# Two graph-attention and expert layers on one core: filled regions without pads, weight packing from the first block, early slots at 14 tiles, VectorE work of layer 1's routing moved, and the first norms in order

## The chip, the cores and the metric

The kernel runs on one core of one Trainium2 chip. The metric is the device time of one execution, in microseconds (us). Engines are named as the profile names them: PE (TensorE, the matmuls; PEld its weight loads), DVE (VectorE), ACT (ScalarE), POOL (GpSimd) and SP (SyncE, which here only issues DMAs). [...]

## The reference

x has N = 2708 rows (nodes) of D = 256 floats, adj is 2708 x 2708 (int32, about 1.2% ones). With E = 8 experts of hidden width 1024 in layer 0 and 512 in layer 1:

```python
# layer 0
h = layernorm(x)
q, k, v = h @ Wq.T + bq, h @ Wk.T + bk, h @ Wv.T + bv
x = x + elu(softmax(where(adj > 0, q @ k.T / 16, -9e15)) @ v)
h = layernorm(x); probs = softmax(h @ Wr + br)
# the two best experts of each row, weighted by their share of the two;
# each expert norms h once more: layernorm(h) * ln_g[e] + ln_b[e], then gelu MLP
x = x + sum_of_two(weight * expert(h))
# layer 1
H = layernorm(x) @ W_fc + b_fc
x = x + softmax(where(adj > 0, (H @ w_src)[:, None] + (H @ w_dst)[None] + b_att, -1e9)) @ H
h = layernorm(x); probs = softmax(h @ gate_w + gate_b)
x = x + sum_of_two(probability * expert(h))        # gelu MLP, no norm of its own
```

## The kernel before

The rows are cut into NT = 22 tiles of 128 (the last has 20 rows). Layer 0's attention takes queries in six blocks of four tiles (`BLOCKS`; the last is 148 rows) and walks the 22 key tiles k in each.

**Layer 0's attention** (`layer0_attention`). At the start the first four tiles are normed (`norm`: statistics on DVE L150 and L151, a scaling L152, a power on POOL L156, and the normed tile L160), transposed and multiplied with Wv (`prepare`), and the queries of block 0 are made (L331). Then for each block and k: `scores` (PE L345, plus the mask, already converted to `apart`, as an additive matmul L351), the exponential on ACT (L356), and the neighbour mask mT on DVE (L357, from the same scores, kept for layer 1); two steps later `attend` (L367). While block b runs, `load_mask` brings the int32 adjacency rows of block b+1 (SP, L254, four buffers, 0.35 MB each) and DVE turns each into `apart` (L257). In block 0 tiles 4 to 21 are normed and prepared on the way.

**Routing** (`Experts.route`, a generator that `Line.step` moves on by one stage at a time, so that a tile's routing runs in small pieces beside the attention of the next block). For each tile: statistics, the norm, a second copy of the row (L694), transposes, gate logits (L701), the two best (L709 to L726), a matmul that counts the rows already given to each expert (L730, L731), and two scatters on POOL that write the 128 rows into the experts' regions of `disp` in DRAM (L748; each row with its token number and weight). In layer 1 `finish` adds the bias to the residual on DVE (L526), and `evict` copies the accumulators alternately on DVE and ACT (L536).

**Experts.** A region's rows are cut into chunks of 128; a chunk is a slot. After `early` = 16 tiles are routed, `begin` places the first 24 slots (`FULL_AFTER`) among chunks that are surely full, and fetches the rows (SP, L889) and the weights (an indirect gather on POOL, L874, ring of four) of three slots ahead. Once all tiles are routed, `place(n, SLOTS)` numbers the rest. A chunk that isn't full must not pick up stale rows: before, each layer had a `disp` of its own, and `place` wrote 128 rows of `nobody` (token N, weight 0) behind the end of each of the eight regions, with register loads on SP:

```python
for e in range(E):
    at = nc.values_load(end[0:1, e : e + 1], ..., engines=(SP,))
    self.other_rows(nc.sync.dma_start(disp[bass.ds(at, P), :], nobody))
```

A slot (`slots`): transpose the rows (L913), first matmul (L933), gelu on ACT (L941), second matmul (L949), bias and weight on DVE (L955, L956), and a scatter with addition into the rows of the result on POOL (L957). The scatter of a slot waits until the one before has landed. 46 slots always run, two and then the rest only if the numbers need them.

**Packing** (`pack_weights`). Per expert the weights are copied DRAM to DRAM into one row per partition (2.2 MB in layer 0, 1.1 MB in layer 1). These copies, the idle rows of `disp` and later the reloading of mT are a list `background`, popped at fixed steps:

```python
if b > 0:
    if k % 5 == 1 and background:
        background.pop(0)()
    line.step()
```

**Order.** SP's instructions stand in the order of the program (`tc.manual_schedule(engines={SP})`); those of the other engines are ordered by a scheduler when the kernel is built. `prepare`, masks and constants compete there.

Of the kernel before, what the change touches and what calls it, by code (L numbers as in the profile page):

```python
# [41 lines left out]
FULL_AFTER = {16: 24}  # L42
# [13 lines left out]
def adj_ffn_kernel(ctx: ExitStack, tc: tile.TileContext, a: dict, out: bass.AP):  # L56
# [32 lines left out]
    part = const.tile([P, 1], F32, name="part")  # L89
    nc.gpsimd.iota(ints[:, :1], pattern=[[0, 1]], base=0, channel_multiplier=1)  # L90
    nc.vector.tensor_copy(part, ints[:, :1])
# [20 lines left out]

    def load_bcast(name, n, c0=0):
        t = const.tile([P, n], F32, name=f"{name}_b")
        nc.gpsimd.dma_start(t, a[name][c0 : c0 + n].partition_broadcast(P))
        return t
# [10 lines left out]
    def load_dmajor(pool, name, n, eng=None):  # L127
        t = pool.tile([P, DC, n], F32, name=f"{name}_w")
        (eng or nc.sync).dma_start(t, a[name].rearrange("(c p) n -> p c n", p=P))
        return t  # L130

    wr = load_dmajor(const, "L0_ffn_Wr", E, nc.gpsimd)
    wg = load_dmajor(const, "L1_ffn_gate_w", E, nc.gpsimd)

    wfc = const.tile([P, DC, D + 1], F32, name="wfc")
    nc.gpsimd.dma_start(wfc[:, :, :D], a["L1_gnn_W_fc"].rearrange("(c p) n -> p c n", p=P))
    for c in range(DC):
        junk = small.tile([P, D], F32, name="junk", bufs=1)
        nc.vector.scalar_tensor_tensor(
            junk, wfc[:, c, :D], 1.0, wdst_b,  # L140
            op0=ALU.mult, op1=ALU.mult, accum_out=wfc[:, c, D : D + 1],
        )

# [80 lines left out]
    def layer0_attention(line):  # L224
        with ExitStack() as scope, ExitStack() as until_last:
# [63 lines left out]
            with tc.tile_pool(name="fold", bufs=1, side="right") as fold:  # L289
# [7 lines left out]
                first = [norm(t) for t in range(4)]  # L297
# [99 lines left out]
            apart = mask_of(0)  # L397
            for t in range(4):
                prepare(t, first[t])
            for _ in load_mask(0, 0, apart):  # L400
                pass
            g = queries(0)
            late, total, accs = [], None, None
            for b, (b0, nb, ts_) in enumerate(BLOCKS):
# [6 lines left out]
                for k in range(NT):  # L411
                    if b == 0:
# [5 lines left out]
                        if k + 4 < NT:  # L418
                            prepare(k + 4, norm(k + 4))

# [19 lines left out]
                    if k >= 2:  # L440
                        next(later_mask, None)
                    if b > 0:
                        if k % 5 == 1 and background:
                            background.pop(0)()
                        line.step()
# [18 lines left out]
    def layer1_attention(mTs, line):  # L464
        with ExitStack() as scope:
# [7 lines left out]
            def load_x2(t):  # L473
                x2s[t] = rows.tile([P, D], F32, name="xin", bufs=9)
                nc.sync.dma_start(x2s[t][: ROWS[t]], xd0[t * P : t * P + ROWS[t], :])

# [45 lines left out]
            def finish(t, raw, total):  # L522
# [3 lines left out]
                nc.vector.tensor_add(x2[:r], x2[:r], bfc_b[:r])  # L526
# [6 lines left out]
            def evict(ts_, accs, total):  # L533
                for j, (t, acc) in enumerate(zip(ts_, accs)):
                    raw = rows.tile([P, D + 1], F32, name="raw", bufs=6)
                    (nc.scalar.copy if j % 2 else nc.vector.tensor_copy)(  # L536
                        raw[: ROWS[t]], acc[: ROWS[t]]
                    )
# [5 lines left out]
            for g, wide in enumerate(GROUPS):  # L544
# [4 lines left out]
                for k in range(NT + (LAG1 if g == 0 else 0)):  # L549
# [14 lines left out]
                    if 0 <= j < wide:  # L564
                        load_x2(ts_[j])
# [47 lines left out]
    class Experts:  # L613
        def __init__(self, layer, hidden, packed_weights, w_gate, gate_bias, own_norm, xd, disp, early):
# [12 lines left out]
            runs = [(0, 0, n // RING), (n, 0, -(-(SURE - n) // RING))]  # L627
            self.number = const.tile([P, SLOTS, 2], F32, name=f"number{layer}")
            number_i = const.tile([P, SLOTS], I32, name=f"number_i{layer}")
            for s0, c0, size in runs:  # L630
                nc.gpsimd.iota(
                    number_i[:, s0 : s0 + size * RING], pattern=[[1, size], [size, RING]], base=c0,
                    channel_multiplier=0,
                )
            s0 = n + runs[1][2] * RING
# [6 lines left out]
            )  # L642

# [30 lines left out]
        def route(self, t, x):  # L674
# [3 lines left out]
            r = ROWS[t]  # L678
            rows2 = [routing.tile([P, DROW], F32, name=f"row{j}") for j in range(2)]
# [14 lines left out]
            nc.vector.tensor_copy(rows2[1][:r, : D + 1], rows2[0][:r, : D + 1])  # L694
# [60 lines left out]
        def place(self, s0, s1):  # L755
# [8 lines left out]
            if all_chunks:  # L764

                end = one.tile([P, E], I32, name="end")
                nc.vector.tensor_add(end, n_e, regions)
                for e in range(E):
                    at = nc.values_load(
                        end[0:1, e : e + 1], min_val=e * CAP, max_val=e * CAP + N,  # L770
                        engines=(mybir.EngineType.SP,),
# [308 lines left out]
```

The softmax here doesn't subtract the row's maximum and nothing guards it: scores larger than these inputs give would overflow.

## Time and profile before

| what | value |
|---|---|
| median of three runs | 1418.88 us (1417.09 to 1419.42) |
| profiled execution | 1421.76 us, its span 1420.0 us |
| PE busy | 1292.1 us (91%), granted clock 0.964 on the mean |
| DVE, ACT, POOL busy | 569.7, 348.9, 435.3 us |
| DMA | 203.01 MB, mean 143 GB/s; SP's queue 107.86 MB, POOL's 93.73 MB |

The span runs from the first to the last instruction. The stages, by the starts and ends of their instructions: until 35 us the first norms, values and queries; until 548 layer 0's attention (blocks end near 137, 228, 322, 419, 505 and 548); until 890 layer 0's slots; from 905 to 1130 layer 1's attention with the routing of its first tiles; then layer 1's slots, in the first of which the last tiles are routed; the last scatter starts at 1404 and the output is copied behind it. PE is busy through most of this, so for a part of the change what matters is whether PE waits at that place, and for what.

### The profile page before, as it was taken

The numbers are of one execution on the slowest core, as the hardware profiler recorded it, in microseconds if no ns is written. First come the engines' busy times: TensorE is split into PE (matmuls) and PEld (weight loads), VectorE is DVE, ScalarE is ACT, GpSimd is POOL, SyncE is SP. The second block draws the span as 40 slices with busy tenths as digits, with TensorE's granted clock in tenths as the row PEclk, the third lists the DMA queues.
The fourth block names the chain that finished last, engine by engine and source line by source line (L and its number), as shares of the span: only waits on it lengthen the run. The fifth ranks groups of instructions, "written<-read, shape, count | busy, mean of one in ns | idle before, by whom it ended". The sixth has DMA issues, their size and how long they took to land. (4 is left out here: it accounts for less than half of the span.)

```text
span 1420.0 us, 21606 instructions
## 1 busy us (share of the span) xinstructions
PE 1292.1 (91%) x7680; PEld 1009.8 (71%) x7680; DVE 569.7 (40%) x2182; ACT 348.9 (25%) x1035; POOL 435.3 (31%) x478
## 2 busy tenths in 40 slices
PE   5999999999999999999999999599989876989872
PEld 3676666666566666999999999478878565878662
DVE  5623744536417264422221222565465543323220
ACT  2322222122112224433333332232001142222120
POOL 5100110110101122543333333431333346555552
PEclk8999999999999999999999999899999978999996
DMA  7601785978727036556686543310221256564664
GB/s 238 207 4 42 205 203 148 248 181 226 190 71 169 23 132 241 156 169 201 203 297 198 155 123 100 81 32 12 65 79 54 73 177 154 114 170 106 183 185 105
DMA packets 108620, 203.01 MB, mean 143 GB/s; under 512 B 25197, under 2 KB 83861, under 8 KB 101933
## 3 DMA queue, kind: packets, MB, share of 16 engines
q1 hardware_dynamic: 76172, 107.86, 27.0%
q0 software_dynamic: 32336, 93.73, 23.0%
q8 instruction: 63, 1.03, 0.3%
q14 instruction: 49, 0.39, 0.1%
HBM read 261.27 MB, written 69.41 MB: 233 GB/s over the span
## 5 line engine op out<-in xcount | busy, mean ns | idle before, releaser
L949 PE MATMUL acc<-ring,hT 128*128 128x256 f32 x1120 | 279.4, 386 | 24.8 <-ACT hT L941 24.8
L933 PE MATMUL mm<-xe,ring 128*128 128x128 f32 x2240 | 286.0, 283 | 9.7 <-DVE xe L923 4.7
L933 PEld LDWEIGHTS mm<-xe,ring 128*128 128x128 f32 x2240 | 275.9, 198 | 23.9 <-issue 14.0
L941 ACT ACTIVATE hT<-mm,ring 128x128 f32<-128x128 f32 x560 | 159.6, 368 | 376.8 <-issue 292.7
L949 PEld LDWEIGHTS acc<-ring,hT 128*128 128x128 f32 x1120 | 200.0, 192 | 55.9 <-ACT hT L941 34.6
L345 PE MATMUL s<-g,xnT 128*128 128x512 f32 (+1 forms) x440 | 215.2, 605 | 4.9 <-DVE mT L357 4.9
L367 PE MATMUL acc<-v,p 128*128 128x257 f32 (+1 forms) x880 | 216.9, 390 | 0.0
L957 POOL DMA_INDIRECT xd<-y,xg x94 | 149.1, 1586 | 173.5 <-DVE y L955 61.1
L517 PE MATMUL acc<-parts,mT 128*128 128x257 bf16 (+1 forms) x1452 | 175.7, 274 | 1.5 <-POOL parts L504 1.0
L955 DVE TENSOR_TENSOR y<-acc,bias 128x256 f32<-128x256 f32 x94 | 39.8, 424 | 339.1 <-PE acc L949 286.6
L367 PEld LDWEIGHTS acc<-v,p 128*128 128x128 f32 (+1 forms) x880 | 159.7, 192 | 19.2
L517 PEld LDWEIGHTS <-mT 128*128 128x128 fp8e4 (+1 forms) x1452 | 137.4, 98 | 30.6 <-issue 9.7
L748 POOL DMA_INDIRECT disp<-row,to x88 | 86.4, 982 | 235.7 <-DVE to L745 139.2
L874 POOL DMA_INDIRECT ring<-L_ffn_packed,weight_row x99 | 104.4, 1055 | 157.9 <-issue 102.9
L156 POOL TENSOR_TENSOR ln_rs<-ln_rs,minus_half 128x2 f32<-128x2 f32 x88 | 66.8, 779 | 245.9 <-DVE ln_rs L152 198.6
L357 DVE TENSOR_SCALAR mT<-s 128x512 fp8e4<-128x512 f32 x110 | 75.4, 687 | 150.4 <-ACT p L356 149.2
L345 PEld LDWEIGHTS s<-g,xnT 128*128 128x128 f32 (+1 forms) x440 | 77.1, 187 | 58.4 <-issue 45.9
L356 ACT ACTIVATE p<-s 128x512 f32<-128x512 f32 x110 | 65.0, 594 | 192.3 <-PE s L351 192.3
L351 PEld LDWEIGHTS <-apart 128*128 128x128 fp8e4 (+1 forms) x440 | 34.2, 99 | 64.5 <-issue 64.5
L257 DVE TENSOR_SCALAR apart<-adj 128x677 fp8e4<-128x677 int32 x80 | 40.9, 515 | 54.2 <-DMA adj<-in_adj_dram 53.7
L913 PE MATMUL tp<-ident,xg 128*128 128x128 f32 x188 | 39.3, 279 | 20.3 <-DMA xg<-disp 17.2
L166 PE MATMUL misc<-ident,xn 128*128 128x128 f32 (+1 forms) x132 | 27.5, 290 | 23.4 <-DVE ln_rs L152 11.6
(183 smaller groups left out, 1067.7 us busy)
## 6 DMA issues: line engine op xcount, KB each, us to landing
adj<-in_adj_dram SPq DMA_DIRECT2D x84, 338.5 KB
L_ffn_packed<-in_L_ffn_W_dram SPq DMA_DIRECT2D x16, 1024.0 KB
xg<-disp SPq DMA_DIRECT2D x99, 129.0 KB
L_ffn_packed<-in_L_ffn_W_dram SPq DMA_DIRECT2D x16, 512.0 KB
neighbours<-mT SPq DMA_DIRECT2D x5, 1408.0 KB
mT<-neighbours SPq DMA_DIRECT2D x5, 1408.0 KB
xin<-in_x_dram SPq DMA_DIRECT2D x42, 128.0 KB
xd<-x SPq DMA_DIRECT2D x42, 128.0 KB
```

Source lines behind the costliest of these rows:

```text
L156: nc.gpsimd.tensor_tensor(rs[:r, 1], rs[:r, 0], minus_half[:r], ALU.pow)
L345: nc.tensor.matmul(ps[:kr, :nb], xnT[:, c, k0 : k0 + kr], g[:, c, :nb], start=(c == 0), stop=False,)
L356: nc.scalar.activation(p[:kr, :nb], ps[:kr, :nb], AF.Exp, scale=1.0 / 16.0)
L357: nc.vector.tensor_scalar(mT[:kr, k, :], ps[:kr, :nb], -BIG / 2, None, ALU.is_gt, saturate=False,)
L367: nc.tensor.matmul(accs[j][:r], p[:kr, j * P : j * P + r], v[:kr, k, :], start=(k == 0), stop=(k == NT - 1),)
L517: nc.tensor.matmul(acc[:r], mT[:, k, q0 : q0 + r], parts[:, k, i], start=(k == 0 and i == 0), stop=(k == NT - 1 and i == 2),)
L748: nc.gpsimd.indirect_dma_start(disp[:], bass.IndirectOffsetOnAxis(ap=to[:r, j : j + 1], axis=0), rows2[j][:r], None,)
L874: nc.gpsimd.indirect_dma_start(w, None, packed[:], bass.IndirectOffsetOnAxis(ap=self.weight_row[:, s : s + 1], axis=0), bounds_check=E * P ...
L933: nc.tensor.matmul(ps[:, i, :], w[:, c * hidden + f * P : c * hidden + (f + 1) * P], xe[:, c, :], start=(c == 0), stop=(c == DC - 1),)
L941: nc.scalar.activation(hT[:, f, :], ps[:, i, :], AF.Gelu, bias=w[:, b1 + f : b1 + f + 1])
L949: nc.tensor.matmul(ps, hT[:, f, :], w[:, w2 + f * D : w2 + (f + 1) * D], start=(f == 0), stop=(f == hc - 1),)
L957: start = nc.gpsimd.indirect_dma_start(xd[:], bass.IndirectOffsetOnAxis(ap=xg.bitcast(I32)[:, D : D + 1], axis=0), y, None, compute_op=ALU ...
```

## The change

Five things, in one version.

1. **Filled regions without pads.** One `disp` serves both layers. In layer 0, `fill(i)` writes `nobody` into tile row i of all eight regions (1.06 MB) on SP: tiles 0 to 3 in block 0 (k from 18), the others one by one when tiles are routed (tile t fills t + 4). The pads are gone. In layer 1 the regions still hold layer 0's rows; `mark_rows` works out which rows of a late slot lie behind the end, and the slot's scatter then takes token and weight from a small tile `to` (slots from 20 on).
2. **Weight packing from the first block.** `background` is popped in block 0 at k = 8, 10, ... 20, and afterwards at k % 5 == 1 as before.
3. **Layer 1's early slots at 14 tiles** instead of 16, 20 slots instead of 24. The second run of slots in both layers is numbered downwards.
4. **VectorE work of layer 1's routing moved.** The residual's bias is added on POOL when the residual is loaded, the row copy goes to ACT, and all evictions go to ACT.
5. **First norms in order.** The first four norms, the loads of the constants and the first mask are put in the order of the program on DVE and POOL too; the loads of the constants are collected in a list and come behind the norms.

```diff
@@ -39,7 +39,7 @@
-FULL_AFTER = {16: 24}
+FULL_AFTER = {16: 24, 14: 20}
@@ -86,9 +86,12 @@
     ints = const.tile([P, 1 + E], I32, name="ints")
-    part = const.tile([P, 1], F32, name="part")
+    part = const.tile([P, 3], F32, name="part")
     nc.gpsimd.iota(ints[:, :1], pattern=[[0, 1]], base=0, channel_multiplier=1)
-    nc.vector.tensor_copy(part, ints[:, :1])
+    nc.vector.tensor_copy(part[:, 0:1], ints[:, :1])
+    nc.vector.tensor_scalar(part[:, 1:2], part[:, 0:1], -1.0, -float(N), op0=ALU.mult, op1=ALU.add)
+    nc.vector.tensor_scalar(part[:, 2:3], part[:, 0:1], float(N), None, ALU.add)
@@ -110,9 +113,14 @@
+    constants = []
...
         t = const.tile([P, n], F32, name=f"{name}_b")
-        nc.gpsimd.dma_start(t, a[name][c0 : c0 + n].partition_broadcast(P))
+        constants.append(
+            partial(nc.gpsimd.dma_start, t, a[name][c0 : c0 + n].partition_broadcast(P))
+        )
@@ -124,22 +132,27 @@
-    def load_dmajor(pool, name, n, eng=None):
+    def load_dmajor(pool, name, n):
         t = pool.tile([P, DC, n], F32, name=f"{name}_w")
-        (eng or nc.sync).dma_start(t, a[name].rearrange("(c p) n -> p c n", p=P))
+        nc.sync.dma_start(t, a[name].rearrange("(c p) n -> p c n", p=P))
...
-    wr = load_dmajor(const, "L0_ffn_Wr", E, nc.gpsimd)
-    wg = load_dmajor(const, "L1_ffn_gate_w", E, nc.gpsimd)
+    wr = const.tile([P, DC, E], F32, name="wr")
+    wg = const.tile([P, DC, E], F32, name="wg")
     wfc = const.tile([P, DC, D + 1], F32, name="wfc")
-    nc.gpsimd.dma_start(wfc[:, :, :D], a["L1_gnn_W_fc"].rearrange("(c p) n -> p c n", p=P))
-    for c in range(DC):
-        junk = small.tile([P, D], F32, name="junk", bufs=1)
-        nc.vector.scalar_tensor_tensor(
-            junk, wfc[:, c, :D], 1.0, wdst_b,
-            op0=ALU.mult, op1=ALU.mult, accum_out=wfc[:, c, D : D + 1],
+    for to, name in ((wr, "L0_ffn_Wr"), (wg, "L1_ffn_gate_w"), (wfc[:, :, :D], "L1_gnn_W_fc")):
+        constants.append(
+            partial(nc.gpsimd.dma_start, to, a[name].rearrange("(c p) n -> p c n", p=P))
...
+    def dst_column():
+        for c in range(DC):
+            junk = small.tile([P, D], F32, name="junk", bufs=1)
+            nc.vector.scalar_tensor_tensor(
+                junk, wfc[:, c, :D], 1.0, wdst_b,
+                op0=ALU.mult, op1=ALU.mult, accum_out=wfc[:, c, D : D + 1],
+            )
@@ -294,7 +307,17 @@
                     load_x(t)
-                first = [norm(t) for t in range(4)]
+                with tc.manual_schedule(
+                    engines={mybir.EngineType.DVE, mybir.EngineType.Pool}
+                ):
+                    first = [norm(t) for t in range(4)]
+                    for start in constants:
+                        start()
+                    apart = mask_of(0)
+                    for _ in load_mask(0, 0, apart):
+                        pass
+                dst_column()
@@ -394,11 +417,8 @@
-            apart = mask_of(0)
...
                 prepare(t, first[t])
-            for _ in load_mask(0, 0, apart):
-                pass
@@ -417,6 +437,8 @@
                             prepare(k + 4, norm(k + 4))
+                    if b == 0 and k >= NT - GROUP:
+                        experts0.fill(k - (NT - GROUP))
@@ -439,9 +461,9 @@
                         next(later_mask, None)
+                    if background and (k >= 8 and k % 2 == 0 if b == 0 else k % 5 == 1):
+                        background.pop(0)()
                     if b > 0:
-                        if k % 5 == 1 and background:
-                            background.pop(0)()
@@ -473,6 +495,11 @@
                 nc.sync.dma_start(x2s[t][: ROWS[t]], xd0[t * P : t * P + ROWS[t], :])
+                return x2s[t]
+            def load_residual(t):
+                x2 = load_x2(t)[: ROWS[t]]
+                nc.gpsimd.tensor_add(x2, x2, bfc_b[: ROWS[t]])
@@ -523,7 +550,6 @@
                 yield
-                nc.vector.tensor_add(x2[:r], x2[:r], bfc_b[:r])
@@ -531,11 +557,9 @@
             def evict(ts_, accs, total):
-                for j, (t, acc) in enumerate(zip(ts_, accs)):
+                for t, acc in zip(ts_, accs):
                     raw = rows.tile([P, D + 1], F32, name="raw", bufs=6)
-                    (nc.scalar.copy if j % 2 else nc.vector.tensor_copy)(
-                        raw[: ROWS[t]], acc[: ROWS[t]]
-                    )
+                    nc.scalar.copy(raw[: ROWS[t]], acc[: ROWS[t]])
@@ -562,7 +586,7 @@
                     if 0 <= j < wide:
-                        load_x2(ts_[j])
+                        load_residual(ts_[j])
@@ -624,15 +648,17 @@
             n = FULL_AFTER[early]
-            runs = [(0, 0, n // RING), (n, 0, -(-(SURE - n) // RING))]
+            size = -(-(SURE - n) // RING)
+            runs = [(0, 0, n // RING, 1), (n, size - 1, size, -1)]
...
             number_i = const.tile([P, SLOTS], I32, name=f"number_i{layer}")
-            for s0, c0, size in runs:
+            for s0, c0, size, step in runs:
                 nc.gpsimd.iota(
-                    number_i[:, s0 : s0 + size * RING], pattern=[[1, size], [size, RING]], base=c0,
-                    channel_multiplier=0,
-                )
-            s0 = n + runs[1][2] * RING
+                    number_i[:, s0 : s0 + size * RING], pattern=[[step, size], [size, RING]],
+                    base=c0, channel_multiplier=0,
+                )
+            s0 = n + size * RING
@@ -640,6 +666,15 @@
+        def fill(self, i):
+            regions_ = self.disp[:IDLE, :].rearrange("(e t p) d -> p e t d", e=E, p=P)
+            start = nc.sync.dma_start(
+                regions_[:, :, i], nobody.unsqueeze(1).to_broadcast([P, E, DROW])
+            )
+            tc.declare_no_dep(start.ins, group=self.groups[0], reason="other rows of disp")
@@ -676,6 +711,8 @@
             r = ROWS[t]
+            if own_norm and t + GROUP <= NT:
+                self.fill(t + GROUP)
@@ -691,7 +728,9 @@
             )
-            nc.vector.tensor_copy(rows2[1][:r, : D + 1], rows2[0][:r, : D + 1])
+            (nc.vector.tensor_copy if own_norm else nc.scalar.copy)(
+                rows2[1][:r, : D + 1], rows2[0][:r, : D + 1]
+            )
@@ -761,17 +800,6 @@
             nc.vector.tensor_copy(n_e, ps[:, :E])
-            if all_chunks:
-                end = one.tile([P, E], I32, name="end")
-                nc.vector.tensor_add(end, n_e, regions)
-                for e in range(E):
-                    at = nc.values_load(
-                        end[0:1, e : e + 1], min_val=e * CAP, max_val=e * CAP + N,
-                        engines=(mybir.EngineType.SP,),
-                        skip_runtime_bounds_check_because="an expert has at most N tokens",
-                    )
-                    self.other_rows(nc.sync.dma_start(disp[bass.ds(at, P), :], nobody))
@@ -809,6 +837,21 @@
                 )
+            marked = all_chunks and not self.own_norm
+            if marked:
+                end = one.tile([P, E], F32, name="end")
+                change_end = one.tile([P, E - 1], F32, name="change_end")
+                passed_end = one.tile([P, n, E], F32, name="passed_end")
+                nc.vector.tensor_add(end, n_e, regions)
+                nc.vector.tensor_sub(change_end, end[:, 1:], end[:, : E - 1])
+                nc.vector.tensor_mul(
+                    passed_end[:, :, : E - 1], passed[:, :, : E - 1],
+                    change_end.unsqueeze(1).to_broadcast([P, n, E - 1]),
+                )
+                nc.vector.tensor_copy(
+                    passed_end[:, :, E - 1 :], end[:, 0:1].unsqueeze(1).to_broadcast([P, n, 1])
+                )
@@ -820,6 +863,8 @@
                 nc.vector.tensor_scalar(self.used, last[:, E - 1 : E], float(s0), None, ALU.add)
+                if marked:
+                    self.mark_rows(s0, passed_end, row)
@@ -850,6 +895,22 @@
                 op0=ALU.mult, op1=ALU.add,
+            )
+        def mark_rows(self, s0, ends, row):
+            n = SLOTS - s0
+            left = self.one.tile([P, n], F32, name="left")
+            self.has = self.one.tile([P, n], I32, name="has")
+            self.instead = self.one.tile([P, n, 2], I32, name="instead")
+            nc.vector.tensor_reduce(left, ends, AX.X, ALU.add)
+            nc.vector.tensor_sub(left, left, row)
+            nc.vector.tensor_scalar(left, left, part[:, 0:1], None, ALU.is_gt)
+            nc.vector.tensor_scalar(self.has, left, -1.0, None, ALU.mult)
+            nc.vector.memset(self.instead, 0)
+            nc.vector.tensor_scalar(
+                self.instead[:, :, 0], left, part[:, 1:2], part[:, 2:3], op0=ALU.mult, op1=ALU.add
@@ -953,10 +1014,20 @@
                 nc.vector.tensor_add(y, ps, bias2)
-                nc.vector.tensor_scalar(y, y, xg[:, D + 1 : D + 2], None, ALU.mult)
+                to = xg.bitcast(I32)[:, D : D + 2]
+                if not own_norm and s >= FULL_AFTER[self.early]:
+                    i = s - FULL_AFTER[self.early]
+                    to = two.tile([P, 2], I32, name="to", bufs=3)
+                    nc.vector.tensor_tensor(
+                        to, xg.bitcast(I32)[:, D : D + 2],
+                        self.has[:, i : i + 1].to_broadcast([P, 2]), ALU.bitwise_and,
+                    )
+                    nc.vector.tensor_tensor(to, to, self.instead[:, i], ALU.bitwise_or)
+                nc.vector.tensor_scalar(y, y, to.bitcast(F32)[:, 1:2], None, ALU.mult)
...
                     xd[:],
-                    bass.IndirectOffsetOnAxis(ap=xg.bitcast(I32)[:, D : D + 1], axis=0),
+                    bass.IndirectOffsetOnAxis(ap=to[:, 0:1], axis=0),
@@ -1013,13 +1084,12 @@
-    disps = [dram.tile([E * CAP + P, DROW], F32, name=f"disp{i}") for i in range(2)]
-    for disp in disps:
-        background.append(partial(nc.sync.dma_start, disp[IDLE:, :], nobody))
+    disp = dram.tile([E * CAP + P, DROW], F32, name="disp")
+    background.append(partial(nc.sync.dma_start, disp[IDLE:, :], nobody))
...
     packed1 = pack_weights("L1_ffn", 512, False)
-    experts0 = Experts(0, 1024, packed0, wr, br_b, True, xd0, disps[0], 16)
-    experts1 = Experts(1, 512, packed1, wg, gb_b, False, xd1, disps[1], 16)
+    experts0 = Experts(0, 1024, packed0, wr, br_b, True, xd0, disp, 16)
+    experts1 = Experts(1, 512, packed1, wg, gb_b, False, xd1, disp, 14)
```

## The prediction, made before the result was known

> **What bounds the kernel now.** I read the slices of the page first, to see where TensorE (PE) is not full.
>
> ```profile
> PE   5999999999999999999999999599989876989872
> DMA  7601785978727036556686543310221256564664
> ```
>
> A slice is 35.5 us. PE is full from the second slice to the 25th, so there only PE work or a small stall can move the end. It has holes at the start, at slice 26 (the step between layers, which the change leaves alone) and from 1000 us on. DMA is full at the start, nearly idle from 60 to 140 us, and full again in stretches to 380 us. Second, PE's waits, by what ended them (line waiting, releaser, us in all, times, longest):
>
> ```profile
> PE acc L949 <- ACT hT L941: 24.8, 41, 10.6
> PE tp L913 <- DMA xg<-disp: 17.2, 8, 5.5
> PE misc L166 <- DVE number L640: 10.4, 1, 10.4
> PE misc L730 <- DVE sel L726: 8.9, 5, 3.4
> PE s L345 <- DVE mT L357: 4.9, 4, 3.0
> ```
>
> Each row belongs to one place. L640 is the wait for the first normed tile, at the start. L357 stands for masks that come late in layer 0's attention. L726 is routing inside layer 1's attention (1000 to 1130 us). About half of L913's, and the single 10.6 us of L949, lie in the first slots of layer 1's experts, which the timeline of PE shows (start, us, instruction, count, idle before it and releaser):
>
> ```profile
> 1133.03 0.41 PE L913 MATMUL tp<-ident,xg 128*128 128x128 f32 x2 [1.65 <-DMA xg<-disp]
> ...
> 1139.35 0.69 PE L913 MATMUL tp<-ident,xg 128*128 128x128 f32 x2 [5.46 <-DMA xg<-disp]
> ...
> 1142.48 0.69 PE L913 MATMUL tp<-ident,xg 128*128 128x128 f32 x2 [1.28 <-DMA xg<-disp]
> ...
> 1143.68 3.67 PE L933 MATMUL mm<-xe,ring 128*128 128x128 f32 x16
> ...
> 1155.17 1.95 PE L933 MATMUL mm<-xe,ring 128*128 128x128 f32 x16
> ...
> 1190.13 3.78 PE L949 MATMUL acc<-ring,hT 128*128 128x256 f32 x8 [10.56 <-ACT hT L941]
> ```
>
> The reader sees 8.4 us of waiting for the first rows, then the same 16 matmuls at 3.67 instead of 1.95 us (half clock after a gap). Last, the table by stretches (length, busy PE, PEld, DVE, ACT, POOL, granted clock, DMA share, GB/s):
>
> ```profile
> 40.00:60.00 20.00, 20.00 (x94) 13.65 (x93) 16.35 (x46) 6.23 (x14) 4.87 (x6) 1.00 0.90 294
> 80.00:100.00 20.00, 20.00 (x92) 13.90 (x91) 4.41 (x8) 5.74 (x13) 0.00 (x0) 1.00 0.01 1
> 200.00:220.00 20.00, 20.00 (x85) 12.71 (x84) 3.77 (x11) 4.36 (x7) 2.71 (x3) 1.00 0.36 76
> 240.00:260.00 20.00, 20.00 (x92) 13.31 (x92) 16.47 (x60) 5.03 (x12) 3.56 (x7) 1.00 1.03 241
> ```
>
> A full DMA moves 241 to 294 GB/s, and there is room between 60 and 140 us.
>
> **The sum** is made against the profiled execution, 1421.76 us (span 1420.0, 1.76 around it); it lies 2.88 above the median of 1418.88.
>
> *A, first norms in order.* Now DVE does six tiles' statistics, all small constants and four mask conversions before L160's first row at 18.36, and PE's first transpose starts at 20.77, queries (L331) at 31.25, scores at 34.90. In the new order the first tile's chain follows its load (first statistics at 6.21): 0.43 + 0.18 + 0.21, seven small constants of about 0.15, a pow of 0.78 on POOL, number casts 0.6, norm 0.41: about 9.6. Tiles 1 to 3 cost about 2.0 each one after another (0.43 + 0.18 + 0.21 + 0.78 + 0.41), and POOL's 2.34 us memset of apart_last stands ahead of tile 1's pow: 9.6 + 6.0 + 2.3 = 18 us. From the fourth tile's transpose to the queries it is 31.25 - 29.38 = 1.9 us, so queries at 20 instead of 31. POOL's eight constant DMAs (0.65 us each by rows of that kind) then stand ahead of tile 4's pow, 5.2 us; tile 4 is needed only after the queries (3.6 us), so 1 to 2 show. PE may also be at half clock there (queries 3.6 longer). I take -8.5; ends -11 and -5.
>
> The row for contention: L160 took 2.27 us at 18.36 beside POOL's memset (17.91 to 20.25), 0.41 when alone. [...]
>
> *B, fills and earlier packing.* Removed: 16 pad writes with their register loads, one idle-row write. Added: 23 fills of 128x8x258 floats, 1.06 MB each, 24.3 MB on SP's queue; and seven background steps (six packs of 2.2 MB, 13 MB) move from blocks 1 and 2 into block 0. The queue is shared with the mask loads (L254), whose conversions (L257) stand in DVE's order ahead of mT (L357), for which PE waits. So I count the bytes that SP issues up to the last mask load of each block, in the order of both kernels: block 0 14.8 MB before, 23.9 after; block 1 27.6 and 51.6; block 2 46.8 and 69.8; block 3 61.8 and 83.5. At 245 GB/s these are 98, 211, 285 and 341 us after. When needed: the conversion stands behind mT number 14 of block 0, 16 of block 1, 14 of block 2, 11 of block 3. With scores from 26 and 4.65 us per step in block 0, 4.13 later, that is 95, 200, 283 and about 365 us. Late by about 2, 10 (not added up: the later includes the earlier) and then 2; POOL's scatters, 0.26 MB a tile, add 4 us. The blocks now take 91, 94, 96 against 87 for the undisturbed block 4, so 20 us are lost already, 4.1, 7.6 and 9.4. I expect about 7 more in blocks 0 and 1, 4 less in 2 and 3: +3; ends -6 (the stalls of blocks 2 and 3 shrink) and +15 (10 us late in block 1, half clock behind it). A scatter of tile t waits for its fill, issued on SP three steps earlier; a fill is 1.06 MB / 245 = 4.3 us, a step is 4.1: hidden, unless SP itself is held.
>
> For the clock: four L345 matmuls took 3.78 us after a gap of 3.02 us, against 1.98 elsewhere. [...]
>
> *C, layer 1's routing.* From DVE go 22 adds (L526, 0.42), 22 row copies (0.29) and 11 evictions (0.43): 20 us of DVE, most of it hidden. PE waits 8.9 us in five waits for sel; each has about two adds, a copy and some evictions in front of it, and DVE sat in L526 for late xin loads (0.77, 0.24, 0.30). I take -5. The adds on POOL, not in the trace, lie between L504's cast of 128x257 (0.40) and its longest memset (2.34); I take 0.78, pow's row, which is nearest in kind. They stand up to six in a batch ahead of scatters (L748), whose landing nobody awaits until the slots start. Six evictions on ACT at 0.37 keep up with PE's 0.41 per tile. Ends -9 (all) and +3 (a batch of 2.34s in front of a pow that routing awaits).
>
> *D, early slots at 14 tiles.* begin() comes a group earlier, so rows and weights of slots 0 to 2 are there when attention ends: L913's 1.65 + 5.46 + 1.28 = 8.4 go, and the half clock behind them (3.67 + 3.03 - 2 x 1.95 = 2.8): 11.2. The 10.56 us stall beside the pads may go too, but then POOL is late next: it is busy without a break from 1165 to 1186 with scatters L748 (about 1.0 each and 0.3 between) and L957, and the number of those behind the first L957 stays at ten. From 1185.88 to 1389.70 it issues 41 L957, 4.97 us each, where PE needs about 4.34. So the end moves by what the first L957 (1156.85) moves. I take -11; ends -7 and -15 (first L957 at 1142 if nothing waits).
>
> *E, numbering and marks.* The second run goes downwards, so up to four weight fetches at the turn fall away; with a fetch the chain's step is about 5.2, without 4.5: -2 taken, ends -3 and 0. Seven DVE instructions for marks once, and two of 0.15 a slot from slot 20 on, stand behind y, hidden by POOL's waits (49 us on y, but 18 on nothing): ends 0 and +3 (a third of 28 x 0.3).
>
> Sum: -8.5 + 3 - 5 - 11 - 2 = -23.5, so 1398.3 profiled, and 2.9 less for the median: **1395**.
>
> **Rivals.** *DMA saturated (slower).* If fills beside packs move fewer bytes per second, masks starve blocks 0 to 2. For it: DMA has little room (69.8 MB of 285 us), and 76 GB/s at share 0.36 (200 to 220 us) is 211 at full; against: the rows at share 1 show 241 and more. The gain of 23.5 is used up when 69.8 MB take 285 + 23.5 = 308 us, below 226 GB/s. At 218 they take 320: 1395 + 35 = 1430. *PE decides the first slots, not POOL:* then the 10.56 and its half clock (2.4) go as well: 1395 - 13 = 1382. *First scatter held, or first norms still late* (three adds, two pairs of L748 and a pow stand before the first L957; a memset ahead of a pow): seven of D or all of A is lost: 1402 to 1404. That the fills do nothing is not a case: 24 MB will show.
>
> **How the numbers follow.** Forecast 0.53, PE decides 0.15, held 0.17, saturated 0.13, and 0.02 for both losses together, near no change. The range runs from 1377 (PE decides and A's and C's better ends, less some) to 1416 (B at +15, D at -7 and A at -5). A difference of 0.2%, 2.8 us, is what can be told from none: faster 0.83, same 0.04, slower 0.13.
>
> **What would show it.** Right: PE's first transpose at 10 to 12 and queries near 20; DMA share over 0.8 from 60 to 230 us and block 1's end near 225 to 235; sel's waits under 5; no L913 wait over 1 us at the start of layer 1's slots, first L957 about 11 us nearer to the end of attention; from there on 4.9 us a slot. Wrong: L357 or L257 waiting over 15 us in blocks 0 and 1, the slots' step over 5.1, or a first L957 that has not moved.

## The result and the profile after

The changed kernel takes 1427.86 us (median of four runs, 1423.27 to 1429.38), the kernel before in the same set 1417.99: ratio 1.0065, 95% interval 1.0038 to 1.0093. It is slower by 0.65%, where 1395 (1377 to 1416) had been forecast. Run again in two other sets, it stood at 1.0119 [1.0076, 1.0161] and 1.0136 [1.0101, 1.0170]. The profiled execution took 1423.27 us, span 1421.5; it is the fastest of the four.

The slices of the page, after (35.5 us each):

```profile
PE   6989899989999999999999999599989978888872
DMA  7999996974707038465677454310221345555453
```

The idle DMA of 60 to 140 us is gone (the third and fourth digits were 0 and 1 and are 9 now), as forecast; PE's row has 8s where it was full. PE's waits, after (line waiting, releaser, us in all, times, longest):

```profile
PE s L368 <- DVE mT L380: 19.8, 9, 5.7
PE mm L994 <- DMA ring<-L_ffn_packed,weight_row: 16.2, 9, 2.7
...
PE misc L769 <- DVE sel L765: 10.8, 3, 7.6
PE mm L994 <- DVE xe L984: 10.2, 3, 8.9
PE misc L740 <- ACT gT L180: 6.6, 4, 4.2
...
PE tp L974 <- DMA xg<-disp: 2.8, 1, 2.8
```

Lines have moved: L368, L380 and L270 are scores, mT and the mask conversions (L345, L357, L257 before), L765 is sel. PE's waits for masks went from 4.9 to 19.8 us, and the waits for ring, xe and gT, 4.7, 4.7 and 0.5 us before, to 16.2, 10.2 and 6.6. VectorE's waits until 420 us, first before, then after:

```profile
DVE apart L257 <- DMA adj<-in_adj_dram: 53.7, 28, 7.4
...
DVE ln_st L150 <- DMA xin<-in_x_dram: 8.3, 4, 5.0
```

```profile
DVE apart L270 <- DMA adj<-in_adj_dram: 74.8, 27, 10.2
DVE ln_st L163 <- DMA xin<-in_x_dram: 26.3, 4, 9.4
```

VectorE waits 39 us longer for loads, with mT behind them in its order. The stages, from starts in three profiles (us; "again" is the profile of the same kernel in another set):

| start of | before | before again | after | after again |
|---|---|---|---|---|
| queries of block 0 | 31.2 | 31.4 | 18.3 | 17.7 |
| first mT of block 0 | 38.8 | 39.0 | 34.0 | 33.3 |
| first mT of block 1 | 141.1 | 141.3 | 141.5 | 142.6 |
| of block 2 | 231.1 | 231.2 | 242.3 | 247.4 |
| of block 3 | 325.6 | 325.9 | 338.2 | 350.0 |
| of block 4 | 421.7 | 422.0 | 427.4 | 439.3 |
| layer 0's slots | 552.8 | 553.1 | 561.4 | 573.9 |
| layer 1's attention | 913.2 | 914.3 | 921.7 | 934.9 |
| first scatter of layer 1's slots | 1156.9 | 1156.6 | 1163.0 | 1178.7 |
| 46th scatter | 1394.3 | 1394.4 | 1391.8 | 1417.4 |
| 48th scatter | 1404.2 | 1403.9 | 1405.9 | 1430.6 |

So 13 us won at the queries are 5 at the first mT, and blocks 0 to 2 turn them into a loss of 13 (24 in the other profile). Block 3 gives some back. Layer 1's attention up to the first scatter, forecast 16 us shorter (C and D together), is 2 us shorter, or 1.5 longer. In the first profile the slots then make up the rest: 228.8 us from the first to the 46th scatter instead of 237.4, so that the changed kernel stands 2.5 us ahead at the 46th; it loses 4 at the last two (14.1 us instead of 10.0). In the other profile the same stretch takes 238.7 us instead of 237.8, and nothing is made up.

### The profile page after: what moved, and what is told of

Its sections match the earlier page's. It is cut to its first block, busy times and chain, and to the rows that moved or that the text cites. A ratio compares the mean times of both kernels' runs of the same rounds, so it can differ in the third digit from the quotient of the medians.

```text
span 1421.5 us, 21616 instructions
## 1 busy us (share of the span) xinstructions
PE 1292.5 (91%) x7680; PEld 1007.0 (71%) x7680; DVE 560.9 (39%) x2192; ACT 367.0 (26%) x1073; POOL 453.1 (32%) x500
## 3 DMA queue, kind: packets, MB, share of 16 engines
q8 instruction: 63, 1.03, 0.3%
## 5 line engine op out<-in xcount | busy, mean ns | idle before, releaser
L994 PE MATMUL mm<-xe,ring 128*128 128x128 f32 x2240 | 282.8, 281 | 26.4 <-DMA ring<-L_ffn_packed,weight_row 16.2
L368 PE MATMUL s<-g,xnT 128*128 128x512 f32 (+1 forms) x440 | 218.7, 614 | 19.8 <-DVE mT L380 19.8
L544 PE MATMUL acc<-parts,mT 128*128 128x257 bf16 (+1 forms) x1452 | 180.3, 278 | 1.6 <-POOL parts L531 1.2
L1028 POOL DMA_INDIRECT xd<-y,xg x66 | 105.3, 1595 | 104.8 <-issue 32.9
L368 PEld LDWEIGHTS s<-g,xnT 128*128 128x128 f32 (+1 forms) x440 | 78.1, 190 | 75.3 <-issue 46.5
L380 DVE TENSOR_SCALAR mT<-s 128x512 fp8e4<-128x512 f32 x110 | 75.5, 687 | 125.7 <-ACT p L379 125.6
L270 DVE TENSOR_SCALAR apart<-adj 128x677 fp8e4<-128x677 int32 x80 | 40.6, 512 | 75.0 <-DMA adj<-in_adj_dram 74.8
L1028 POOL DMA_INDIRECT xd<-y,to x28 | 43.7, 1562 | 60.6 <-DVE to L1022 40.9
```

Source lines behind the costliest of these rows:

```text
L368: nc.tensor.matmul(ps[:kr, :nb], xnT[:, c, k0 : k0 + kr], g[:, c, :nb], start=(c == 0), stop=False,)
L380: nc.vector.tensor_scalar(mT[:kr, k, :], ps[:kr, :nb], -BIG / 2, None, ALU.is_gt, saturate=False,)
L544: nc.tensor.matmul(acc[:r], mT[:, k, q0 : q0 + r], parts[:, k, i], start=(k == 0 and i == 0), stop=(k == NT - 1 and i == 2),)
L994: nc.tensor.matmul(ps[:, i, :], w[:, c * hidden + f * P : c * hidden + (f + 1) * P], xe[:, c, :], start=(c == 0), stop=(c == DC - 1),)
L1028: start = nc.gpsimd.indirect_dma_start(xd[:], bass.IndirectOffsetOnAxis(ap=to[:, 0:1], axis=0), y, None, compute_op=ALU.add,)
```

## The experiments

All ratios are to the kernel before in the same set of runs. Besides the time, two distances tell the places apart: from the first mT to layer 0's first slot (514.0 in the kernel before), and from the start of layer 1's attention to the first scatter of its slots (242.3 and 243.7). A profile is one execution; the kernel before repeats these within 1.5 us, the changed one within 13 us in layer 0 (+13.4, +26.6 and +23.8 in three profiles) and 2.5 in layer 1. The second distance says less than that: only_first has layer 1's instructions in the same order on every engine as the kernel before, and yet 247.1. So a difference under 5 us in that column, from one profile each, shows nothing by itself. In most other versions the scheduler also put VectorE's instructions in a somewhat different order.

| run | ratio [95%] | layer 0 against 514.0 | layer 1 to first scatter |
|---|---|---|---|
| after_again | 1.0119 [1.0076, 1.0161] | +26.6 | 243.8 |
| after_third | 1.0136 [1.0101, 1.0170] | +23.8 | 242.8 |
| only_first | 0.9980 [0.9954, 1.0005] | -1.9 | 247.1 |
| no_early_pack | 1.0146 [1.0100, 1.0193] | +31.9 | 241.2 |
| no_fill | 0.9957 [0.9934, 0.9981] | +6.2 | 242.1 |
| early16 | 1.0211 [1.0161, 1.0260] | +29.6 | 249.4 |
| no_moves | 1.0139 [1.0096, 1.0182] | +26.5 | 243.4 |
| fix_ab | 1.0127 [1.0083, 1.0171] | +22.0 | 236.9 |
| no_fill_no_pack | 0.9912 [0.9874, 0.9950] | -0.6 | 240.2 |
| best1 | 0.9912 [0.9880, 0.9945] | +0.1 | 238.1 |
| best2 | 0.9871 [0.9833, 0.9909] | +0.1 | 235.7 |
| fix_abt | 1.0107 [1.0059, 1.0154] | +25.2 | 238.7 |
| fill_wide | 1.0172 [1.0139, 1.0206] | +19.8 | 242.2 |
| few_fills | 1.0060 [1.0036, 1.0085] | +14.6 | 244.1 |
| best3 | 0.9808 [0.9782, 0.9835] | -1.2 | 231.2 |
| best3_early16 | 0.9946 [0.9923, 0.9969] | +0.4 | 242.6 |
| best3_no_fix | 0.9905 [0.9871, 0.9939] | +2.3 | 242.5 |

**Layer 0: one part alone, or one part undone.**

only_first: the kernel before with the norms' order alone. 

> The kernel before with the fifth part alone (first four norms, constants and first mask in program order). Theory 1, the order is a gain that the full version loses again in layer 0's blocks: queries near 18 us, first mT 5 us or more earlier than 38.8, and the time 5 to 9 us below the kernel before. Rival, the first mask conversion was what held the blocks and not the norms: queries early, but the first block ends where it did, time within 2 us of the kernel before.

no_early_pack:
```diff
-if background and (k >= 8 and k % 2 == 0 if b == 0 else k % 5 == 1):
-    background.pop(0)()
 if b > 0:
+    if k % 5 == 1 and background:
+        background.pop(0)()
```


> The changed kernel with packing as before (from block 1, every five steps). Theory 1a, it is the 13 MB moved into block 0 that starve the mask and x loads: block 0 keeps its gain and the time falls by 8 to 12 us against the changed kernel. Theory 1b, it is the 24 MB of fills: the same bytes come later, blocks 1 to 3 lose what block 0 gains, and the time stays within 3 us of the changed kernel.

no_fill: both calls of `fill` and the marks out, two `disp` and the pads back. 

> The changed kernel with two disps and pads as before, without fills and marks. Theory 1b (fills saturate the DMA): blocks 1 and 2 lose at most half of their 12 us and the time falls by 10 us or more against the changed kernel. Theory 1a (early packing does it): block 0 and 1 lose the same as in the changed kernel, time lower by less than 4 us. If the pads' stall of 10 us was real and costs time, it comes back here and takes up to 10 us of the gain.

no_fill_no_pack: both of these. 

> The changed kernel without fills and marks and with packing as before: first norms, early slots at 14, VectorE moves and numbering are left. Theory 1 (layer 0 loses its lead only through the added and the earlier transfers): layer 0's blocks run as in the kernel with the first norms alone, fifth block's end 7 us before that of the kernel before, and the time 8 to 12 us below the kernel before. Rival (the first norms' lead is lost in any case, or the loss lies in layer 1): within 4 us of it.

The order of the norms is a gain that the interval just leaves unclear (1423.91 against 1427.46), less than theory 1 had. It is 4.5 us ahead at the first mT and 6.4 at layer 0's slots, and 1.5 at layer 1's first scatter; where the rest went isn't known. Without fills the loss falls from 13 to 27 us to 6; without the earlier packing but with fills it is not smaller (+31.9); without both it is gone (-0.6). So theory 1b holds over 1a: the fills are the main cost. The earlier packing costs 7 us where there are no fills (+6.2 against -0.6; one profile each, and the intervals of the two ratios overlap) and none that shows where there are. The pads that came back in no_fill brought no stall of 10 us with them.

**What of the fills costs.** few_fills:
```diff
-if own_norm and t + GROUP <= NT:
+if own_norm and t + GROUP < 8:
     self.fill(t + GROUP)
```


> The changed kernel with only the first eight of the 23 fills (8.5 MB of 24.3; the others are left out, which these inputs do not need, but others would). Theory 1, the loss goes with the bytes in each block: blocks 0 and 1 as slow as in the changed kernel (block 2 starts 12 us or more after it does in the kernel before), blocks 2 and 3 as fast as without fills, the time 5 to 10 us below the changed kernel. Rival, it is the waiting of SP and of the scatters for a fill: the loss in blocks 2 and 3 stays as far as the early packing makes it.

fill_wide: source tile [32, 4 * 258], destination "(e t p j) d -> p e t (j d)" with j = 4. 

> The changed kernel with fills of the same bytes in packets of 4128 instead of 1032 bytes (a tile of 32 partitions with four rows each as the source). Theory 1c, the fills cost by packets (74 ns each on the mean, 96 us of all sixteen engines): their engine time falls to 60 to 75 us and the time by 4 to 10 us. Theory 1d, they cost by bytes: the engine time and the time stay within 3 us of the changed kernel.

With a third of the fills the loss goes from +23.8 to +14.6 and the time by 9.7 us, and what is left is in blocks 0 and 1, where the eight fills are: block 2 starts at 245.7 (248.0 in after_third), but from there to block 4 it takes 185.8 us against 189.9 (186.4 in no_fill). The loss goes with the transfers, as theory 1 has it. fill_wide fits neither theory. Until 540 us the packets of 21 fills took 84.5 us of the sixteen engines instead of 99 (a quarter as many, 4128-byte packets of 252 ns on the mean against 73), and blocks 1 to 4 lost much less (fifth block's end 509.8 against 523.0), but block 5 took 59.5 us instead of 49.2, and POOL now waits for the fills themselves (until 560 us):

```profile
POOL disp L796 <- DMA disp<-nobody: 64.7, 4, 23.0
```

The time rose by 6.5 us; layer 0's slots took 369.6 us instead of 361.3. The fills don't land later after their issue (8.7 us in the median against 10.9 in after_third); they are issued later. The scatter at 240.81 waited 22.3 us for a fill that SP issued at 231.60, behind mask loads that stood waiting for VectorE's conversions (139.1 us of such waits from 130 to 560 us, 3.2 in after_third). VectorE has a different order of instructions in this version, so it doesn't tell what the packets' size alone is worth.

**Layer 1.** early16: `experts1 = Experts(..., 16)` in the changed kernel. 

> The changed kernel with layer 1's early slots at 16 tiles and 24 slots again. Theory 2, the earlier begin only swaps the wait for the first rows (8.4 us) for a wait of the routing for residuals queued behind the three weight gathers (7.6 us and half clock): time within 3 us of the changed kernel, the 7.6 us wait for sel gone and L974's (rows) back. Rival, the earlier begin is worth its 11 us: time 8 us or more above the changed kernel.

no_moves: L526's add, the row copy and `evict` as before. 

> The changed kernel with the residual's add, the row copy and half of the evictions on VectorE again. Theory 3, the moves put new waits in the place of the old ones (ACT's gT behind row copies, 4.2 us; POOL behind late residuals): the 4.2 us wait for gT goes, the time is within 4 us of the changed kernel's. Rival, the moves are a gain of 5 us as forecast: 5 us or more slower than the changed kernel.

fix_ab:
```diff
-x3 = rows.tile([P, D], F32, name="x1")
+x3 = rows.tile([P, D], F32, name="x1", bufs=7)      # x1 too
-j = k - (NT - 1 - wide if wide > GROUP else NT // 2)
+j = k - (NT - 1 - wide if wide > GROUP else 2)
```


> The changed kernel with seven buffers instead of three for the row tile x1/x3 and residuals of the small groups loaded from the third step of a group instead of the twelfth. Theory 2, layer 1's last group waits because stores and residual loads stand behind begin's three weight gathers (3.5 MB, about 14 us): the 7.6 us wait for sel falls below 2 and the first slots' scatter comes 6 to 9 us earlier against the start of layer 1's attention; time 5 to 9 us below the changed kernel. Rival, it was another wait (POOL's power behind adds, ACT's copies): less than 3 us.

The timeline of the changed kernel shows the wait that took the place of the old one (PE, then VectorE, then SP; start, us, instruction, idle before it and releaser):

```profile
1134.12 2.47 PE L544 MATMUL acc<-parts,mT 128*128 128x257 bf16 x18
1144.18 0.19 PE L769 MATMUL misc<-sel,before 128*128 128x8 bf16 x1 [7.59 <-DVE sel L765]
```

```profile
1138.79 0.48 DVE L554 SCALAR_TENSOR_TENSOR x<-raw,z,xin 128x256 f32<-128x256 f32 x1 [9.77 <-DMA xd<-x]
```

```profile
1125.32 1.80 SPq L950 DMA_DIRECT2D xg<-disp  x3
1127.59 0.04 SPq L719 DMA_DIRECT2D xd<-x  x1
1127.71 0.90 SPq L497 DMA_DIRECT2D xin<-xd  x2
```

begin issues three weight gathers (from 1124.06, 1.2 MB each) and three row fetches; the stores of x (L719) and the residuals' loads (L497) come right behind and land near 1139. x3 has three buffers, so VectorE waits at L554 for a store to leave its buffer, and the gate and sel of another tile stand behind that. fix_ab took sel's waits from 11.2 us (after_again) to 4.0 and the first scatter 4 to 7 us nearer; its time did not follow (1.0127 against 1.0119 in the same set), since layer 0's loss of 22 us and its spread lie over it. early16's first scatter comes 6 to 8 us later than the changed kernel's, and its ratio is 0.8 to 1.5 points higher (11 to 21 us, part of it layer 0's spread): its rival held, not theory 2. no_moves fits theory 3: 1.0139 against 1.0119, no clear difference; the waits for gT fell from 6.5 to 0.5 us and those for sel rose from 11.2 to 16.7 (after_again against no_moves).

**Without layer 0's loss.** best1 (no_fill_no_pack with fix_ab's two edits): 

> The same, with seven buffers for x1/x3 and the early residual loads. Theory 2: 5 to 8 us less than without them, through the wait for sel (7.6 us) in layer 1's last group; 14 to 18 us below the kernel before. Rival, the scatter chain takes it back: the same time as without them.

best2 (best1 with the moves undone): 

> The same as the last one, with the residual's add, the row copy and half of the evictions on VectorE again. Theory 3 (the moves are worth nothing, ACT's and POOL's own waits take their place): within 3 us of the last one. Rival, they are worth 5 us: 5 us slower.

best3 (best2; wfc's load on SP and its two products at the end of block 0):
```diff
-                dst_column()
...
                     if b == 0 and k == NT - 1:
+                        nc.sync.dma_start(
+                            wfc[:, :, :D], a["L1_gnn_W_fc"].rearrange("(c p) n -> p c n", p=P)
+                        )
+                        dst_column()
```


> The kernel without fills and early packing, with first norms, early slots at 14, seven buffers for x1/x3 and early residual loads, VectorE's work left on VectorE, and the load of wfc and its two products moved behind block 0. Theory 5, the lead of 13 us at the queries falls to 5 at the first mT because VectorE stands in the products that wait for wfc, with the next norms and mT behind them: first mT 3 to 6 us earlier than 34, and the time 15 to 22 us below the kernel before. Rival, the norms of tiles 5 to 7 and the masks hold it: first mT within 1.5 us of 34.

best3_early16 and best3_no_fix undo one thing each in best3: 14 tiles with 20 slots become 16 with 24, and fix_ab's two edits go.

> The fastest version with layer 1's early slots at 16 tiles and 24 slots again. Step D of the prediction, measured without layer 0's loss: if the earlier begin is worth its 11 us once stores and residuals don't stand behind its gathers, the first scatter comes 9 to 12 us later against the start of layer 1's attention (240 to 243 instead of 231 us) and the time is 7 to 12 us higher. Rival, the buffers and the early residual loads are the gain and the earlier begin is not: within 3 us.

> The fastest version with three buffers for x1/x3 and residual loads from the twelfth step, as in the changed kernel. Theory 2: the wait for sel of 7 to 9 us in layer 1's last group is back, first scatter 6 to 10 us later against the start of layer 1's attention and the time 4 to 9 us higher. Rival: within 3 us.

This pair settles step D. Waits of PE from 900 to 1200 us, in best3, best3_early16 and best3_no_fix:

```profile
PE misc L769 <- DVE sel L765: 8.3, 4, 3.4
```

```profile
PE tp L985 <- DMA xg<-disp: 12.5, 7, 4.3
```

```profile
PE misc L769 <- DVE sel L765: 19.0, 6, 9.7
```

With the earlier begin and the room for stores the first scatter comes after 231.2 us, with either undone after 242.5: the earlier begin is worth 11 us there, and without the two edits that is lost again, with 10.7 us more of waits for sel. Their ratios are 1.4 and 1.0 points above best3's, 20 and 14 us, more than was expected of either: best3_early16 also takes 204.8 us instead of 197.7 from the sixth to the 46th scatter, and best3_no_fix 3.5 more in layer 0. best1 and best2 differ by 4 us with overlapping intervals, so the moves to POOL and ACT are worth nothing that these runs show, and may cost. best1 and no_fill_no_pack have the same ratio, so there the rival held for the time, though the first scatter came 2 us earlier; without the moves the same two edits gave 11. best3's first mT is at 31.4, 2.8 us earlier than best2's and 2.6 before the 34 of theory 5: a little short of its 3 us, and beyond the rival's 1.5. The time is 24.6 us below the kernel before, more than its 15 to 22. best3 is faster than best2 by more than the 2.8 us; 4.5 us lie in layer 1 before the first scatter and are not explained.

best3 is the fastest version: 1396.11 us against 1420.72 of the kernel before, ratio 0.9808. It has neither fills nor marks, nor the early packing and the moves.

**The tail.** fix_abt is fix_ab with `to` in eight buffers instead of three. 

> The changed kernel with fills, seven buffers for x1/x3, early residual loads and eight buffers instead of three for the small tile to of the marks. Theory 4 (to of a slot waits for the scatter three slots before, and xe of the next slot stands behind it on VectorE): the 8.9 us wait for xe at the 47th slot goes, from the 46th to the 48th scatter 9 to 10 us instead of 13 to 14. Rival, the distance is the numbering's weight fetches: unchanged. The time stays above the kernel before, by 0 to 10 us, for layer 0's loss is untouched.

 The changed kernel's 47th slot, VectorE and PE:

```profile
1391.11 0.16 DVE L1022 TENSOR_TENSOR to<-xg,has 128x2 int32<-128x2 int32 x1 [4.25 <-DMA xd<-y,to]
...
1391.38 0.75 DVE L984 COPY xe<-tp 128x256 f32<-128x256 f32 x2
...
1391.86 6.70 PE L994 MATMUL mm<-xe,ring 128*128 128x128 f32 x32 [8.87 <-DVE xe L984]
```

A tile of two numbers with three buffers waits for the scatter three slots back, and the copy that PE needs stands behind it. With eight buffers the stretch from the 46th to the 48th scatter took 9.1 us instead of the 13.2 of fix_ab (10.0 in the kernel before): theory 4 holds.

before_again and after_again are profiles of both kernels from one set, after_third is one of the changed kernel from another. 

> The kernel before, for a profile beside the others of this set: block 2 starts near 231 us, layer 1's attention to the 46th scatter lasts about 477 us.

 

> The changed kernel itself, so that the other runs of this set have it beside them: 0.5 to 1.0% above the kernel before. If the DMA moves less per second than in the first profile, the start of block 2 comes later than 242 us, and the time is the later by about the same.

 

> The changed kernel once more, as the reference of this set: 0.6 to 1.2% above the kernel before.

 The profile of the kernel before no longer has the 10.56 us stall (PE's waits from 905 to 1220 us):

```profile
PE acc L949 <- ACT hT L941: 3.7, 8, 1.1
```

and yet its first, sixth and 46th scatter start at 1156.6, 1190.4 and 1394.4, as they did with the stall (1156.9, 1191.2, 1394.3).

## Why the prediction was wrong

**A** was right in its working and wrong in its end. Queries came at 18.3 (forecast 20), but the term went on to the scores as if nothing stood between. VectorE's order had the products that wait for wfc (2.35 us) and the norms of later tiles ahead of the first mT, and with two score buffers PE stopped:

```profile
27.18 0.42 DVE L152 SCALAR_TENSOR_TENSOR junk<-wfc,L_gnn_w_att_b 128x256 f32<-128x256 f32 x1 [2.35 <-DMA wfc<-in_L_gnn_W_fc_dram]
...
33.96 0.69 DVE L380 TENSOR_SCALAR mT<-s 128x512 fp8e4<-128x512 f32 x1
```

```profile
34.70 2.08 PE L368 MATMUL s<-g,xnT 128*128 128x512 f32 x2 [5.73 <-DVE mT L380]
```

5 us of the 8.5 were left at the first mT, and in only_first 1.5 at layer 1's first scatter. I had seen that POOL's constants moved behind the norms, and not who waits for the last of them.

**B is the step that failed**: +3 (at worst +15) was forecast, 13 to 27 measured. The bytes were about right (51.6 MB counted up to the last mask load of block 1; SP's queue had moved 54.3 when block 2 began) and so was the rate: from 60 to 220 us the changed kernel's DMA moved 242 GB/s on the mean of eight rows (236 in after_again), where 245 was taken. What failed was to turn lateness into PE time, the term "about 7 more in blocks 0 and 1". They became 16 us longer (22 again): the count had the mask loads alone, while the x loads of block 0 stand in the same queue (26.3 us of VectorE's waits instead of 8.3), and each late tile stops VectorE with mT, routing and the next conversions behind it. PE's waits for mT in blocks 0 and 1, in the kernel before (34 to 231 us) and in the changed one (34 to 242):

```profile
PE s L345 <- DVE mT L357: 0.6, 1, 0.6
```

```profile
PE s L368 <- DVE mT L380: 15.4, 6, 5.7
```

The 5.7 is A's; no_fill_no_pack has 6.0 us there, 5.5 of them A's. So the prediction's own sign of being wrong, more than 15 us, came about. The stretch 160 to 180 us before and after (columns as in the prediction):

```profile
160.00:180.00 20.00, 20.00 (x95) 13.57 (x94) 13.05 (x53) 3.36 (x11) 3.93 (x6) 1.00 0.96 242
```

```profile
160.00:180.00 20.00, 17.15 (x70) 10.79 (x71) 14.66 (x54) 3.36 (x8) 3.48 (x6) 0.91 1.03 269
```

PE has lost 2.9 us there and part of its clock. Before, the DMA was nearly as full there and PE lost nothing, after a stretch, from 60 to 140 us, with the DMA at a share of 0.05. So the outcome of the rival that I named for the slower side came, masks that starve the first blocks, but not from its cause: I had it come from a rate below 226 GB/s, and it came at 242. That its 1430 lies near the measured 1427.86 is luck. In blocks 2 and 3 the forecast of -4 was met by -5.5 in the first profile (+1 again).

**C** was nothing: the old waits for sel (8.9 us in five) shrank to 3.2 in two, and new ones came. ACT copies rows in its order, so gT stands behind copies that wait for later tiles (4.2 us once, 6.6 in all). An add on POOL takes 0.73 us against 0.42 on VectorE, 1.7 times as long, and near the 0.78 taken from pow's row.

**D** was right in size (11 us, best3 against best3_early16) and wrong in place: "rows and weights are there" held (the waits for xg fell from 17.2 us to 2.8), but the gathers went out while the last group's stores and loads needed the same DMA (share 0.88, 315 GB/s from 1124 to 1139 us), which nothing in the term counted. As made, the change takes 241.3 to 243.8 us to the first scatter, and the kernel before 242.3 and 243.7. That the 10.56 us stall doesn't set the end of the slots was right: before_again lacks it and ends no earlier. The 4.97 us a slot were miscounted: from 1185.88 to 1389.70 there are 41 scatters but 40 steps, so 5.10.

**E**: from the sixth to the 46th scatter 194 to 200 us instead of 203 to 204, more than the -2 forecast. best3_early16 has the downward numbering with 24 early slots and took 204.8, best3 197.7 with 20, so the direction alone saves nothing that shows; it is 14 tiles with 20 slots that saves, and which of the two isn't known. The price of "hidden" for the marks was 0 to 3; to's buffers made it 4 at the last slots.

In the range, the terms named for the upper end, 12, 4 and 3.5 us on 1395, make 1415, not 1416.

## What to carry to other kernels

When bytes are added to a queue that an engine waits on, cost each late transfer by everything behind it in the waiting engine's order, not by the lateness of one kind of load: here VectorE's waits for loads until 420 us went from 62.0 to 101.1 us, and PE's for mT in blocks 0 and 1 from 0.6 to 15.4. From 60 to 220 us the DMA's share here was 1.03 on the mean (0.38 before), and PE was busy for 148.7 of these 160 us where it had been for 159.4; so look at the share before you put transfers beside loads that must be on time. A prefetch issued earlier can be paid by the transfers that it now overtakes: look for the small stores and loads issued just after it, and for buffers that they hold (here VectorE waited 9.77 us for a store, and PE 7.59 us for sel). A tiny tile with few buffers, read by a scatter, can hold up the engine that writes it: one of two numbers with three buffers held VectorE for 4.25 us here, and PE for 8.87.

## What the runs showed of the hardware

The clock after a gap: in the changed kernel, scores after gaps of 1.82 and 2.40 us ran at full speed (two matmuls in 1.12 us, granted clock 1.00), after 3.76, 4.40 and 5.73 us at about half (four in 3.56 and 3.60, two in 2.08; granted clock 0.56, 0.54 and 0.50 on the mean of these rows). Other rows don't follow the length of the gap. The granted clock was also low after gaps of 3.02 and 2.66 us (kernel before, 0.50 on the mean from 369.85 to 373.60 and 0.61 from 1277.46 to 1281.00) and of 2.96 and 2.80 us (changed kernel, 0.50 from 1091.25 to 1094.00 and from 1183.52 to 1186.50), and it was 1.00 after one of 3.41 us (kernel before, from 1049.92 to 1052.50). So the length of one gap doesn't decide it here.

The changed kernel differs by 12 us between two sets (1427.86 and 1439.95) and by 13 us in layer 0, where its DMA is full (+13.4 and +26.6; share 1.03 on the mean from 60 to 220 us in both profiles), while the kernel before repeats within 1 us there in its two profiles. That the full DMA is the reason isn't shown.
